# One-hot rows of two edge pairs built by one comparison against a row in PSUM, in a three-layer relational GNN on one Trainium2 core

## Chip, cores and metric

The kernel runs on one core of one Trainium2 chip. The metric is the device time of one execution, in microseconds. The engines are named as in the profile: PE (TensorE), DVE (VectorE), ACT (ScalarE), POOL (GpSimd) and SP (SyncE); each runs its own instructions in program order and waits on semaphores that other engines or DMAs raise.

## The reference

A graph of 6250 nodes with 256 features and 100000 edges, sorted by target node, with three edge types; three layers, then a layer norm of input plus result.

```
ew = edge_attr @ edge_w + edge_b                       # (100000, 256)
inv_cnt[r] = 1 / max(number of edges of type r into the node, 1)
for l in range(3):
    residual = x
    msg = relu(x[src] * ew)
    out = 0
    for r in range(3):
        h = segment_sum(msg * (edge_type == r), dst)   # (6250, 256)
        out += (h * inv_cnt[r]) @ weights[l, r]
    out += x @ roots[l] + biases[l]
    x = residual + relu(out)
result = layernorm(x_in + x)
```

## The kernel before

**Pairs, quads and steps.** The edges are cut into 391 *pairs* of two times 128 edges; two neighbouring pairs are a *quad* and share one 128x1024 tile of gathered rows, `xs`. A layer walks over its pairs in a fixed order, one pair at a *step* `it`, and the order of every engine's instructions is written out by hand in that loop. There is no scheduler. At step `it` the loop emits, among others and in this order:

- the two gathers of pair `it + 9`: `gather_pair` (L1054), indirect DMAs that POOL issues, 128 rows each; 2346 over the three layers. The quads take turns in eight buffers for `xs`, the *rooms*: the first gather of a quad waits until the quad eight earlier has been reduced;
- `reduce` of pair `it` (L687 where a span is reduced turned, else L695): one-hot times rows, summed over edges into a PSUM bank of `h_pool`, which has two banks;
- `make_ew` (L634, edge weights of a later quad on PE into PSUM `ew_p`, which holds the bias already: `seed_ew`, L621 on ACT), `weigh` (L656 on DVE, `xs` times `ew_p`, and L657 on ACT, the relu), each once in two steps;
- now and then the root term `x @ roots` of a block of 128 nodes: 49 in a layer, one every six steps or more. `root_turn` (L728, two transposes on PE into `r_p`), two steps later `root_turned` (L732, ACT copies them to `t_s`), three steps later `root_mul` (L736, two products on PE into the other half of `r_p`), six steps later `root_keep` (L739, DVE adds the bias);
- `node_mul` and `node_end` (L754, L785, L788) where the sums of a block of nodes are complete: products with the layer's weights into `o_p`, and the update of `x_all`;
- every second step `one_hot` of the quad that is reduced two steps later (L669): four DVE comparisons of 128x120, each of the row `iota_w` (places 0 to 39, three times) in SBUF with one column of `seg`. In the first layer ACT makes a bfloat16 copy `oh_b` (L673);
- last, `add` (L723): DVE adds the finished span of the step before from its bank of `h_pool` to the sums `acc`. Only then can PE open that bank again, with the `reduce` of the step that follows.

**Start and end.** A first part (the *look*) loads the inputs, and finds out whether the edges are sorted; a flag and two branches (L1171 and L1174) choose `ordered_path`, which is described here, or `general_path`, which does not run with these inputs. In `ordered_path` ACT's queue then loads the edge weights' matrix (`ew_sb`) and bias (`seed`, and a third copy, `left`), DVE makes `bias` in bfloat16 parts from `left`, and DVE (one memset, L518) and ACT (two activations, L520) set `acc` to zero. The last layer ends with the norm and the writes of `out` by SP (L808), and then the second branch.

Of the kernel before, what the change touches and what calls it, by code (L numbers as in the profile page):

```python
# [442 lines left out]
def ordered_path(ctx, tc, x, attr_laid, A, weights, roots, biases, edge_w, edge_b, out, src, src_i, seg, place_i, consts, x_root,  # L443
# [6 lines left out]
    nc = tc.nc  # L450
    P = 128
    N, D = x.shape
    E = src.shape[0]
    L, R = weights.shape[:2]
# [3 lines left out]
    U = T // 2  # L458
    assert OCT * A == P
    DC = D // P  # L460
    WK = R * WIN
# [4 lines left out]
    for u, (lo, hi) in enumerate(zip(least, most)):  # L466
# [4 lines left out]
        else:  # L471
            reach.append((0, RING - 1))
    ident, ones, iota_w = consts

# [4 lines left out]
    big = ctx.enter_context(tc.tile_pool(name="big", bufs=1))  # L479
    ew_sb = big.tile([P, 2, D], F32, name="ew_sb")  # L480
    nc.vector.memset(ew_sb, 0.0)
    for j in range(OCT):
        nc.scalar.dma_start(ew_sb[j * A:(j + 1) * A, j % 2, :], edge_w)
    seed = big.tile([P, 2, D], F32, name="seed")
    for i in range(2):
        nc.scalar.dma_start(seed[:, i, :], edge_b[None, :].to_broadcast([P, D]))
    bias = big.tile([PARTS, 2, D], BF, name="bias")
    with tc.tile_pool(name="bias_s", bufs=1) as bias_s:
        left = bias_s.tile([P, D], F32, name="left")
        nc.scalar.dma_start(left, edge_b[None, :].to_broadcast([P, D]))  # L490
        row = bias_s.tile([P, 1], F32, name="row")
        nc.vector.tensor_copy(row, node_i)
        is_row = bias_s.tile([P, PARTS], F32, name="is_row")
        part = bias_s.tile([P, D], BF, name="part")
        rows_of = bias_s.tile([P, D], F32, name="rows_of")
        nc.vector.memset(rows_of, 0.0)
        for k in range(PARTS):
            nc.vector.tensor_scalar(is_row[:, k:k + 1], row, float(k), None, op0=ALU.is_equal)
            nc.vector.tensor_copy(part, left)
            nc.vector.tensor_sub(left, left, part)  # L500
            nc.vector.scalar_tensor_tensor(rows_of, part, is_row[:, k:k + 1], rows_of, op0=ALU.mult, op1=ALU.add)
        for i in range(2):
            nc.vector.tensor_copy(bias[:, i, :], rows_of[:PARTS, :])

# [8 lines left out]
    nc.vector.memset(eps, EPS)  # L513
    full_ones = big.tile([P, P], BF, name="full_ones")
    nc.vector.memset(full_ones, 1.0)
    for c in range(DC + 1):
        if c < DC // 2:
            nc.vector.memset(acc[:, c], 0.0)  # L518
        else:
            nc.scalar.activation(acc[:, c].rearrange("p r n -> p (r n)"),  # L520
                                 zero.to_broadcast([P, R * (ASIDE + 2 * P + WIN)]), AF.Copy)
# [5 lines left out]
    src_r = big.tile(list(src_i.shape), I32, name="src_r")  # L527
    src_e = big.tile([P, 2 * FIRST], I32, name="src_e")
    came = big.tile([P, 2 * FIRST, P], F32, name="came")
    came_i = came.bitcast(I32)  # L530

# [55 lines left out]
    def layer(l, r_sb, b_sb, ats, early, pools):  # L587
# [56 lines left out]
        def complete(q):  # L644
            for k in pairs_of(q):

                rest = (r_pool if k else o_pool).tile([P, 2, D], F32, name="r_p" if k else "o_p")
# [17 lines left out]
        def one_hot(q):  # L665
            ohs[q] = edge.tile([P, 4, WK], F32, name="oh", bufs=3)
            n = 2 * len(pairs_of(q))
            for t in reversed(range(n)):
                nc.vector.tensor_scalar(ohs[q][:, t, :].rearrange("p (r w) -> p r w", r=R), iota_w[:, :, :WIN], seg[:, 4 * q + t:4 * q + t + 1], None,  # L669
                                        op0=ALU.is_equal)  # L670
# [54 lines left out]
        def root_turn(c):  # L725
            rs[c] = r_pool.tile([P, 2, DC * P], F32, name="r_p")
            for d in range(DC):
                nc.tensor.transpose(rs[c][:, 0, d * P:(d + 1) * P], x_all[:, c, d * P:(d + 1) * P], ident)  # L728

        def root_turned(c):  # L730
            t_ss[c] = edge.tile([P, DC, P], F32, name="t_s", bufs=1)
            nc.scalar.activation(t_ss[c], rs[c][:, 0, :], AF.Copy)  # L732

        def root_mul(c):
            for d in range(DC):
                nc.tensor.matmul(rs[c][:, 1, :], t_ss[c][:, d, :], r_sb[:, d, :], start=(d == 0), stop=(d == DC - 1))  # L736

        def root_keep(c):
            nc.vector.tensor_add(x_root[:, at_root[c], :], rs[c][:, 1, :], b_sb)  # L739
            if l == L - 1:  # L740
                nc.vector.tensor_add(x_all[:, c, :], x_all[:, c, :], x0s[c])
# [180 lines left out]
WIN = 40  # L922
# [137 lines left out]
def kernel(ctx, tc, x, src, dst, edge_attr, edge_type, weights, roots, biases, edge_w,  # L1060
# [28 lines left out]
    flag = keep.tile([1, 1], I32, name="flag")  # L1089

    x_root = keep.tile([P, ROOTS, D], F32, name="x_root")

    with tc.tile_pool(name="look", bufs=1) as look, tc.tile_pool(name="look_p", bufs=2, space=PSUM) as look_p, \
# [5 lines left out]
        typ_raw = look.tile([P, TC], I32, name="typ_raw")  # L1099
        nc.sync.dma_start(typ_raw, type_laid)  # L1100

        limits = look.tile([1, 2, U], F32, name="limits")
# [68 lines left out]
    with tc.If(unordered == 0):  # L1171
        ordered_path(tc, x, attr_laid, edge_attr.shape[1], weights, roots, biases, edge_w, edge_b, out, src, src_i, seg, place_i,
                     (ident, ones, iota_w), x_root, first_rows, node_i)
    with tc.If(unordered > 0):  # L1174
        general_path(tc, x, src, dst, edge_attr, edge_type, weights, roots, biases, edge_w, edge_b, out)
# [49 lines left out]
```

## Time and profile before

| | |
|---|---|
| median of 3 runs | 2961.4 us (2960.73 to 2961.57) |
| profiled execution, its own time | 2962.46 us |
| its span in the profile | 2960.2 us |
| mean granted TensorE clock | 0.97 |
| busy share of the span | PE 88%, DVE 68%, ACT 51%, POOL 75% |

Each group row of the profile gives line, engine, operation, output tile <- input tiles, shape and count, then total busy us and mean ns of one, then the engine's idle time ahead of these instructions and what ended it. A timeline row gives start, duration, the instruction, and in square brackets the idle time before it and what ended it. A row of windows gives a stretch, its length, the busy time of PE, PE's weight loads, DVE, ACT and POOL with their counts, then the mean granted clock, the DMA share and GB/s.

### The profile page before, as it was taken

To read this page: it belongs to the slowest core of one execution; us is meant where nothing else is said; L and a number is where in the kernel's file an instruction comes from. 1 tells how busy PE (TensorE), PEld (TensorE's weight loads), DVE (VectorE), ACT (ScalarE), POOL (GpSimd) and SP (SyncE) were. 2 spreads that over 40 slices of the span, in tenths; PEclk is the share of its full clock that TensorE was granted. 3 is DMA by queue.
4 is the path that set the end of the run, shared out by engine and by line. 5 is a ranking of instruction groups with operands and counts; after the bars stand their busy time and mean duration, and the time that the engine had idled before them with its cause. 6 is when DMAs were issued, how large, how long until landed. Compare 5 with 4: busy or idle time off the path is not lost. (4 is left out here: it accounts for less than half of the span.)

```text
span 2960.2 us, 43407 instructions
## 1 busy us (share of the span) xinstructions
PE 2591.9 (88%) x13712; PEld 1782.6 (60%) x13712; DVE 1998.2 (68%) x4910; ACT 1503.8 (51%) x1911; POOL 2228.8 (75%) x2355
## 2 busy tenths in 40 slices
PE   5999999999998878888889998778888888999876
PEld 2666677677765545556666666454555666666644
DVE  6666677778775555566767776545666777888864
ACT  4666656556565444454444444435444444444443
POOL 7777777777777777777777777777777777777776
PEclk9999999999999999999999999889999999999998
DMA  5444444444444444444444444444444444444443
GB/s 168 151 143 136 148 124 125 127 130 130 127 134 128 132 116 120 129 122 124 127 125 130 130 132 129 136 132 125 126 133 133 135 133 132 139 137 137 129 125 97
DMA packets 173705, 387.39 MB, mean 131 GB/s; under 512 B 43594, under 2 KB 79068, under 8 KB 173468
## 3 DMA queue, kind: packets, MB, share of 16 engines
q0 software_dynamic: 112608, 307.65, 36.4%
q1 hardware_dynamic: 53280, 68.50, 7.2%
q10 hardware_dynamic: 7580, 8.37, 1.0%
q8 instruction: 113, 1.85, 0.3%
q14 instruction: 124, 1.02, 0.1%
HBM read 364.89 MB, written 19.46 MB: 130 GB/s over the span
## 5 line engine op out<-in xcount | busy, mean ns | idle before, releaser
L1054 POOL DMA_INDIRECT xs<-x_mid,src_r x1540 | 1460.5, 948 | 469.1 <-issue 363.4
L657 ACT ACTIVATE xs<-xs 128x1024 f32<-128x1024 f32 (+1 forms) x585 | 615.7, 1053 | 1301.0 <-DVE xs L656 1296.5
L656 DVE TENSOR_TENSOR xs<-ew_p,xs 128x1024 f32<-128x1024 f32 (+1 forms) x585 | 711.4, 1216 | 676.7 <-DMA xs<-x_mid,src_r 429.8
L1054 POOL DMA_INDIRECT xs<-in_x_dram,src_io x770 | 732.0, 951 | 234.6 <-issue 192.3
L695 PEld LDWEIGHTS h_p<-oh,xs 128*128 128x128 f32 x5160 | 669.7, 196 | 251.9 <-issue 123.8
L695 PE MATMUL h_p<-oh,xs 128*128 128x120 f32 x5160 | 734.3, 287 | 86.4 <-issue 34.5
L634 PE MATMUL ew_p<-ew_sb,at 64*128 64x512 f32 x2346 | 687.6, 662 | 95.8 <-ACT ew_p L621 92.3
L669 DVE TENSOR_SCALAR oh<-iota_w,seg_o 128x120 f32<-128x120 f32 x2346 | 622.9, 327 | 0.0
L687 PE MATMUL h_p<-xs,oh 128*120 128x256 f32 x2088 | 570.9, 407 | 22.9 <-issue 7.8
L621 ACT ACTIVATE ew_p<-seed 128x1024 f32<-128x1024 f32 x582 | 588.9, 1012 | 0.0
L754 PE MATMUL o_p<-w_sb,acc 128*128 128x256 f32 (+1 forms) x1728 | 440.7, 391 | 28.2 <-DVE x_root L785 24.2
L687 PEld LDWEIGHTS h_p<-xs,oh 128*120 128x120 f32 x2088 | 363.1, 191 | 162.8 <-issue 48.1
L723 DVE TENSOR_TENSOR acc<-h_p,acc 128x240 f32 (+1 forms) x732 | 323.7, 442 | 173.2 <-PE o_p L754 69.6
L754 PEld LDWEIGHTS o_p<-w_sb,acc 128*128 128x128 f32 (+1 forms) x1728 | 309.3, 191 | 152.0 <-DVE x_root L785 62.7
L634 PEld LDWEIGHTS ew_p<-ew_sb,at 64*128 64x128 f32 x2346 | 181.9, 189 | 224.9 <-ACT ew_p L621 121.1
L785 DVE SCALAR_TENSOR_TENSOR x_root<-o_p,inv,x_root 128x256 f32<-128x256 f32 (+1 forms) x432 | 207.0, 479 | 28.3 <-PE o_p L754 21.6
L736 PE MATMUL r_p<-r_sb,t_s 128*128 128x256 f32 x588 | 160.1, 395 | 26.1 <-ACT t_s L732 25.8
L771 ACT ACTIVATE acc<-zero_o 128x768 f32<-128x768 f32 (+1 forms) x150 | 140.2, 934 | 15.3 <-PE o_p L754 14.7
L673 ACT ACTIVATE oh_b<-oh 128x480 bf16<-128x480 f32 x196 | 116.3, 594 | 56.1 <-DVE oh L669 55.2
L728 PEld LDWEIGHTS r_p<-ident_o,x_all 128*128 128x128 f32 x294 | 30.9, 144 | 169.0 <-DVE x_root L739 116.7
L736 PEld LDWEIGHTS r_p<-r_sb,t_s 128*128 128x128 f32 x588 | 103.0, 192 | 47.6 <-ACT t_s L732 36.4
L728 PE MATMUL r_p<-ident_o,x_all 128*128 128x128 f32 x294 | 65.4, 305 | 69.3 <-DVE x_root L739 69.1
(110 smaller groups left out, 940.8 us busy)
## 6 DMA issues: line engine op xcount, KB each, us to landing
at<-in_attr_laid_dram SPq DMA_DIRECT2D x147, 256.0 KB
xs<-x_mid,src_r POOLq DMA_INDIRECT x1540, 2.8
xs<-in_x_dram,src_io POOLq DMA_INDIRECT x770, 2.8
x_mid<-x_all SPq DMA_DIRECT2D x96, 128.0 KB
x_all<-in_x_dram ACTq DMA_DIRECT2D x8, 768.0 KB
x<-in_x_dram SPq DMA_DIRECT2D x48, 128.0 KB
out_dram<-x_all SPq DMA_DIRECT2D x48, 128.0 KB
w_sb<-in_L_gnn_weights_dram SPq DMA_DIRECT2D x3, 768.0 KB
```

The costliest lines, as they stand in the source:

```text
L621: nc.scalar.activation(ew_ps[q][:, :n], seed[:, None, :, :].to_broadcast([P, n, 2, D]), AF.Copy)
L634: nc.tensor.matmul(ew_ps[q][:, k].rearrange("p i d -> p (i d)"), at[half, :], ew_sb[half].rearrange("p i d -> p (i d)"), start=False, stop ...
L656: nc.vector.tensor_mul(there, ew_ps[q][:, pairs.start:pairs.stop], there)
L657: nc.scalar.activation(there, there, AF.Relu)
L669: nc.vector.tensor_scalar(ohs[q][:, t, :].rearrange("p (r w) -> p r w", r=R), iota_w[:, :, :WIN], seg[:, 4 * q + t:4 * q + t + 1], None, o ...
L687: nc.tensor.matmul(h_p[:WK, :D], ohs[u // 2][:, t, :], xs[u // 2][:, u % 2, i, :], start=(i == 0 and first), stop=(i == 1 and closes(u)), ...
L695: nc.tensor.matmul(h_p[:, d * WK:(d + 1) * WK], xs[u // 2][:, u % 2, i, d * P:(d + 1) * P] if d < DC else full_ones, (ohs if d < DC else o ...
L723: nc.vector.tensor_tensor(there, h_ps[span][:, :CH * WK].rearrange("p (c r w) -> p c r w", c=CH, r=R), there, op=ALU.add)
L736: nc.tensor.matmul(rs[c][:, 1, :], t_ss[c][:, d, :], r_sb[:, d, :], start=(d == 0), stop=(d == DC - 1))
L754: nc.tensor.matmul(o_p[:n, j, :], acc[:, d, r, slot:slot + n], w_sb[:, r * DC + d, :], start=(d == 0), stop=(d == DC - 1))
L785: nc.vector.scalar_tensor_tensor(root, o_p[:n, j, :], inv[:n, c, r:r + 1], root, op0=ALU.mult, op1=ALU.add)
L1054: nc.gpsimd.indirect_dma_start(out=xs[:, u % 2, i, :], out_offset=None, in_=x_rows[:, :], in_offset=bass.IndirectOffsetOnAxis(ap=src_i[:, ...
```

## The change

Four things are edited.

1. **One-hots.** `one_hot` makes the one-hot rows of a quad by a single `tensor_tensor` of 128x480 in place of four `tensor_scalar` of 128x120. Its first operand is a row of places, broadcast over the four blocks, that lies in PSUM; its second is four columns of `seg`, broadcast over the places. For the row, `r_pool` becomes one fixed bank, `r_bank`: 256 columns are `r_p`, the next 120 are `places_p`, copied once from `iota_w`. The transposes and the product of a root term now use the same 256 columns one after the other, and the few `node_mul` and `complete` products that took an `r_p` tile take `o_p`, but for one.
2. **Early loads.** `ew_sb` and `seed` are loaded in the look, ahead of the flag; the third copy of the bias is gone, and `bias` is made from `seed` with the tile `came` as scratch.
3. **Zeros.** All three parts of `acc` are set to zero by ACT.
4. **Hint.** In the last layer's last pair a hint names the second branch by its label, `general`.

```
-    ident, ones, iota_w = consts
+    ident, ones, iota_w, ew_sb, seed = consts
...
-    ew_sb = big.tile([P, 2, D], F32, name="ew_sb")
-    nc.vector.memset(ew_sb, 0.0)
-    for j in range(OCT):
-        nc.scalar.dma_start(ew_sb[j * A:(j + 1) * A, j % 2, :], edge_w)
-    seed = big.tile([P, 2, D], F32, name="seed")
...
-        left = bias_s.tile([P, D], F32, name="left")
-        nc.scalar.dma_start(left, edge_b[None, :].to_broadcast([P, D]))
...
+        rest = seed[:, 0, :] if k == 0 else left
+        nc.vector.tensor_scalar(is_row[:, k:k + 1], row, float(k), None, op0=ALU.is_equal)
+        nc.vector.tensor_copy(part, rest)
+        nc.vector.tensor_sub(left, rest, part)
...
     for c in range(DC + 1):
-        if c < DC // 2:
-            nc.vector.memset(acc[:, c], 0.0)
-        else:
-            nc.scalar.activation(acc[:, c].rearrange("p r n -> p (r n)"),
-                                 zero.to_broadcast([P, R * (ASIDE + 2 * P + WIN)]), AF.Copy)
+        nc.scalar.activation(acc[:, c].rearrange("p r n -> p (r n)"),
+                             zero.to_broadcast([P, R * (ASIDE + 2 * P + WIN)]), AF.Copy)
...
     r_pool = ctx.enter_context(tc.tile_pool(name="r_p", bufs=1, space=PSUM))
+    r_bank = r_pool.tile([P, 4 * P], F32, name="r_p")
+    r_p, places_p = r_bank[:, :D], r_bank[:, None, D:D + WK]
+    nc.vector.tensor_copy(r_bank[:, D:D + WK].rearrange("p (r w) -> p r w", r=R), iota_w[:, :, :WIN])
...
-            for t in reversed(range(n)):
-                nc.vector.tensor_scalar(ohs[q][:, t, :].rearrange("p (r w) -> p r w", r=R), iota_w[:, :, :WIN], seg[:, 4 * q + t:4 * q + t + 1], None,
-                                        op0=ALU.is_equal)
+            nc.vector.tensor_tensor(ohs[q][:, :n], places_p.to_broadcast([P, n, WK]),
+                                    seg[:, 4 * q:4 * q + n, None].to_broadcast([P, n, WK]), op=ALU.is_equal)
...
         def root_turn(c):
-            rs[c] = r_pool.tile([P, 2, DC * P], F32, name="r_p")
             for d in range(DC):
-                nc.tensor.transpose(rs[c][:, 0, d * P:(d + 1) * P], x_all[:, c, d * P:(d + 1) * P], ident)
+                nc.tensor.transpose(r_p[:, d * P:(d + 1) * P], x_all[:, c, d * P:(d + 1) * P], ident)
...
-                nc.tensor.matmul(rs[c][:, 1, :], t_ss[c][:, d, :], r_sb[:, d, :], start=(d == 0), stop=(d == DC - 1))
+                nc.tensor.matmul(r_p, t_ss[c][:, d, :], r_sb[:, d, :], start=(d == 0), stop=(d == DC - 1))
...
-            o_p = o_ps[c, part] = (r_pool if part == 1 and c < 2 else o_pool).tile(
-                [P, 2, D], F32, name="r_p" if part == 1 and c < 2 else "o_p")
+            o_p = o_ps[c, part] = r_p[:, None, :] if part == 1 and c == 0 else o_pool.tile([P, 2, D], F32, name="o_p")
...
+            if l == L - 1 and it == U - 1:
+                tc.mark_branch_hint_location("general")
...
+        for i in range(2):
+            nc.scalar.dma_start(seed[:, i, :], edge_b[None, :].to_broadcast([P, D]))
+        for j in range(OCT):
+            nc.scalar.dma_start(ew_sb[j * A:(j + 1) * A, j % 2, :], edge_w)
...
-    with tc.If(unordered > 0):
+    with tc.If(unordered > 0, label="general"):
```

Three places show what moves. The first is DVE in the first layer, around a root product: `L669` of before is the group of four comparisons, `L659` of after the single one; `L723` and `L713` are the `add`, `L656` and `L647` the `weigh`; `PE_49` is the semaphore that PE raises. Before:

```order
L723 TENSOR_TENSOR acc<-h_p,acc 128x9x40 [waits PE_49]
L669 TENSOR_SCALAR oh<-iota_w,seg_o 128x120 x4
L723 ISA
L723 TENSOR_TENSOR acc<-h_p,acc 128x9x40 [waits DVE_49,PE_49]
L656 TENSOR_TENSOR xs<-ew_p,xs 128x1024 [waits DMASW1_49,DMASW2_49,DMASW0_49,DMASW3_49,PE_49,Activation_49]
L716 TENSOR_LOAD place_i
L723 ISA
L723 TENSOR_TENSOR acc<-h_p,acc 128x9x40 [waits DVE_49,PE_49]
L669 TENSOR_SCALAR oh<-iota_w,seg_o 128x120 x4
```

And after:

```order
L713 TENSOR_TENSOR acc<-h_p,acc 128x9x40 [waits PE_49]
L659 TENSOR_TENSOR oh<-r_p,seg_o 128x480 [waits PE_49]
L713 ISA
L713 TENSOR_TENSOR acc<-h_p,acc 128x9x40 [waits DVE_49]
L647 TENSOR_TENSOR xs<-ew_p,xs 128x1024 [waits DMASW2_49,DMASW1_49,DMASW3_49,DMASW0_49,Activation_49]
L706 TENSOR_LOAD place_i
L713 ISA
L713 TENSOR_TENSOR acc<-h_p,acc 128x9x40 [waits DVE_49,PE_49]
L659 TENSOR_TENSOR oh<-r_p,seg_o 128x480 [waits PE_49]
```

The order is the same, but a one-hot waited for nothing before, and now waits for PE: the first of the two for the transposes of a root term (L717), the second for its product (L725). Over the program 137 one-hots wait for transposes and 147, one for each root term, for a product.

The second place is PE at a root product in the first layer (`L736` before, `L725` after), which stands between the end of one `reduce` and the start of the next. Before:

```order
L695 LDWEIGHTS full_ones
L695 MATMUL h_p<-oh_b,full_ones 128x120
L736 MATMUL r_p<-r_sb,t_s 128x256 [waits Activation_49]
L736 MATMUL r_p<-r_sb,t_s 128x256
L695 MATMUL h_p<-oh,xs 128x120 [waits DMASW2_49,DVE_49]
```

And after:

```order
L685 LDWEIGHTS full_ones
L685 MATMUL h_p<-oh_b,full_ones 128x120
L725 MATMUL r_p<-r_sb,t_s 128x256 [waits Activation_49]
L725 MATMUL r_p<-r_sb,t_s 128x256
L685 MATMUL h_p<-oh,xs 128x120 [waits DMASW2_49,DVE_49,PE_49]
```

Nothing moved on PE. The `reduce` in the last row waits for an `add` on DVE, as before; that `add` now stands behind a one-hot that waits for the product in the row above.

The third place is ACT's queue at the start. Before, the loads stood behind the flag and the branch:

```order
L1098 DMA dst_raw<-in_dst_laid_dram 128x782
L1170 TENSOR_LOAD flag [waits DVE_49]
L1171 COMPARE_AND_BRANCH
L486 DMA seed<-in_L_gnn_edge_b_dram 128x256 [waits DMAHW0_49,DVE_49,DMAHW3_49,PE_49,Pool_49]
```

And after:

```order
L1092 DMA dst_raw<-in_dst_laid_dram 128x782
L1097 DMA seed<-in_L_gnn_edge_b_dram 128x256 x2
L1099 DMA ew_sb<-in_L_gnn_edge_w_dram 32x256 [waits DVE_49]
L1099 DMA ew_sb<-in_L_gnn_edge_w_dram 32x256
```

The loads of `seed` and `ew_sb` moved ahead of the flag and wait only for the memset of `ew_sb`.

More of the change, by code (lines that the diff above doesn't have):

```diff
@@ L479, in ordered_path @@
     big = ctx.enter_context(tc.tile_pool(name="big", bufs=1))
-    ew_sb = big.tile([P, 2, D], F32, name="ew_sb")
-    nc.vector.memset(ew_sb, 0.0)
-    for j in range(OCT):
-        nc.scalar.dma_start(ew_sb[j * A:(j + 1) * A, j % 2, :], edge_w)
-    seed = big.tile([P, 2, D], F32, name="seed")
-    for i in range(2):
-        nc.scalar.dma_start(seed[:, i, :], edge_b[None, :].to_broadcast([P, D]))
-    bias = big.tile([PARTS, 2, D], BF, name="bias")
-    with tc.tile_pool(name="bias_s", bufs=1) as bias_s:
-        left = bias_s.tile([P, D], F32, name="left")
-        nc.scalar.dma_start(left, edge_b[None, :].to_broadcast([P, D]))
[L491 to L503, printed above, removed]
@@ new lines, in ordered_path @@
+    src_r = big.tile(list(src_i.shape), I32, name="src_r")
+    src_e = big.tile([P, 2 * FIRST], I32, name="src_e")
+    came = big.tile([P, 2 * FIRST, P], F32, name="came")
+    came_i = came.bitcast(I32)
+    full_ones = big.tile([P, P], BF, name="full_ones")
+    nc.vector.memset(full_ones, 1.0)
+    bias = big.tile([PARTS, 2, D], BF, name="bias")
+    scratch = came.rearrange("p t e -> p (t e)")
+    left, rows_of = scratch[:, :D], scratch[:, D:2 * D]
+    row, is_row = scratch[:, 2 * D:2 * D + 1], scratch[:, 2 * D + 1:2 * D + 1 + PARTS]
@@ new lines, in ordered_path @@
+    part = came.bitcast(BF).rearrange("p t e -> p (t e)")[:, 6 * D:7 * D]
+    nc.vector.tensor_copy(row, node_i)
+    nc.vector.memset(rows_of, 0.0)
+    for k in range(PARTS):
+        rest = seed[:, 0, :] if k == 0 else left
+        nc.vector.tensor_scalar(is_row[:, k:k + 1], row, float(k), None, op0=ALU.is_equal)
+        nc.vector.tensor_copy(part, rest)
+        nc.vector.tensor_sub(left, rest, part)
+        nc.vector.scalar_tensor_tensor(rows_of, part, is_row[:, k:k + 1], rows_of, op0=ALU.mult, op1=ALU.add)
@@ L505, in ordered_path @@
+    for i in range(2):
+        nc.vector.tensor_copy(bias[:, i, :], rows_of[:PARTS, :])
     x_all = big.tile([P, NT, D], F32, name="x_all")
@@ L645, in complete @@
             for k in pairs_of(q):
-                rest = (r_pool if k else o_pool).tile([P, 2, D], F32, name="r_p" if k else "o_p")
+                rest = o_pool.tile([P, 2, D], F32, name="o_p")
                 for i in range(2):
@@ L725, in root_turn @@
         def root_turn(c):
-            rs[c] = r_pool.tile([P, 2, DC * P], F32, name="r_p")
             for d in range(DC):
-                nc.tensor.transpose(rs[c][:, 0, d * P:(d + 1) * P], x_all[:, c, d * P:(d + 1) * P], ident)
+                nc.tensor.transpose(r_p[:, d * P:(d + 1) * P], x_all[:, c, d * P:(d + 1) * P], ident)
         def root_turned(c):
             t_ss[c] = edge.tile([P, DC, P], F32, name="t_s", bufs=1)
-            nc.scalar.activation(t_ss[c], rs[c][:, 0, :], AF.Copy)
+            nc.scalar.activation(t_ss[c].rearrange("p d e -> p (d e)"), r_p, AF.Copy)
         def root_mul(c):
             for d in range(DC):
-                nc.tensor.matmul(rs[c][:, 1, :], t_ss[c][:, d, :], r_sb[:, d, :], start=(d == 0), stop=(d == DC - 1))
+                nc.tensor.matmul(r_p, t_ss[c][:, d, :], r_sb[:, d, :], start=(d == 0), stop=(d == DC - 1))
         def root_keep(c):
-            nc.vector.tensor_add(x_root[:, at_root[c], :], rs[c][:, 1, :], b_sb)
+            nc.vector.tensor_add(x_root[:, at_root[c], :], r_p, b_sb)
             if l == L - 1:
@@ L1089 @@
     flag = keep.tile([1, 1], I32, name="flag")
+    ew_sb = keep.tile([P, 2, D], F32, name="ew_sb")
+    seed = keep.tile([P, 2, D], F32, name="seed")
+    A = edge_attr.shape[1]
     x_root = keep.tile([P, ROOTS, D], F32, name="x_root")
@@ L1172 @@
         ordered_path(tc, x, attr_laid, edge_attr.shape[1], weights, roots, biases, edge_w, edge_b, out, src, src_i, seg, place_i,
-                     (ident, ones, iota_w), x_root, first_rows, node_i)
-    with tc.If(unordered > 0):
+                     (ident, ones, iota_w, ew_sb, seed), x_root, first_rows, node_i)
+    with tc.If(unordered > 0, label="general"):
         general_path(tc, x, src, dst, edge_attr, edge_type, weights, roots, biases, edge_w, edge_b, out)
```

7 lines of the change are left out of this document (1 added, 6 removed).

## The prediction

> **What bounds the kernel now.** I read the page's busy shares first, then the groups of POOL, its waits, three windows, and the first and the last gather.
>
> ```profile
> span 2960.2 us, 43407 instructions
> PE 2591.9 (88%) x13712; PEld 1782.6 (60%) x13712; DVE 1998.2 (68%) x4910; ACT 1503.8 (51%) x1911; POOL 2228.8 (75%) x2355
> L1054 POOL DMA_INDIRECT xs<-x_mid,src_r x1540 | 1460.5, 948 | 469.1 <-issue 363.4
> L1054 POOL DMA_INDIRECT xs<-in_x_dram,src_io x770 | 732.0, 951 | 234.6 <-issue 192.3
> ```
>
> ```profile
> POOL xs L1054 <- issue: 562.1, 1845, 0.3
> ```
>
> ```profile
> 500.00:600.00 100.00, 94.97 (x609) 69.89 (x608) 77.98 (x189) 60.35 (x76) 75.70 (x80) 1.00 0.44 128
> 900.00:1000.00 100.00, 84.39 (x486) 56.90 (x482) 47.32 (x110) 47.37 (x59) 75.63 (x81) 0.93 0.45 129
> 2700.00:2800.00 100.00, 89.66 (x517) 65.53 (x514) 83.28 (x217) 49.07 (x63) 75.94 (x80) 1.00 0.46 132
> ```
>
> ```profile
> 3.81 1.12 POOL L1054 DMA_INDIRECT x_root<-in_x_dram,src_f  x1 [1.44 <-DMA src_f<-in_src_laid_dram]
> 2944.28 0.95 POOL L1054 DMA_INDIRECT xs<-x_mid,src_r  x1 [0.30 <-issue]
> 2954.73 0.34 SPq L808 DMA_DIRECT2D out_dram<-x_all  x1
> ```
>
> By busy share PE leads with 88% and POOL has 75%, but POOL's idle time is all of one kind: 0.3 us of issue between one gather and the next, 1845 times. A gather of 0.949 us and 0.30 us of issue are 1.25 us, and 100 us hold 80 of these in every window, whether PE is busy for 84 or 95 us and DVE for 47 or 83. From 3.81 to 2944.28 us stand 2345 periods of 1.254 us (2940.5 / 2345). So POOL is at its limit from end to end, and the span is 3.8 us of head, 2940.5 us of gathers, and 15.9 us from the start of the last gather to the end. What another engine gains in between is worth nothing; what it loses costs nothing until POOL has to wait for a room. So the second question is how much margin the rooms have, from the last product of the reduce that frees a room to the first gather that uses it, eight quads later (pairs counted along the order):
>
> ```profile
> 477.94 0.66 PE L695 MATMUL h_p<-oh,xs 128*128 128x120 f32 x4
> 501.48 0.95 POOL L1054 DMA_INDIRECT xs<-in_x_dram,src_io  x1 [0.30 <-issue]
> 815.85 0.66 PE L695 MATMUL h_p<-oh,xs 128*128 128x120 f32 x4
> 825.05 0.95 POOL L1054 DMA_INDIRECT xs<-in_x_dram,src_io  x1 [0.30 <-ACT xs L657]
> ```
>
> At 500 us the margin is 501.48 - 478.60 = 22.9 us; at 825 us it is 825.05 - 816.51 = 8.5 us. In the first layer PE falls behind POOL by 14 us in 320 us, and 8.5 us is the least margin of that stretch. That is what this change has to be held against.
>
> **The change part by part.** *The one-hots, and their new wait.* The places of the quads lie in the same bank as the root term's results, and the one-hot of a step in which a root product stands now waits for that product. Today it waits for nothing. One such place, in the first layer:
>
> ```profile
> 640.80 1.06 DVE L669 TENSOR_SCALAR oh<-iota_w,seg_o 128x120 f32<-128x120 f32 x4
> 641.78 0.52 DVE L723 TENSOR_TENSOR acc<-h_p,acc 128x360 f32 x1
> 644.67 1.08 PE L736 MATMUL r_p<-r_sb,t_s 128*128 128x256 f32 x4
> 645.60 0.60 PE L695 MATMUL h_p<-oh,xs 128*128 128x120 f32 x4
> 644.45 1.22 DVE L656 TENSOR_TENSOR xs<-ew_p,xs 128x1024 f32<-128x1024 f32 x1 [2.15 <-DMA xs<-in_x_dram,src_io]
> 645.59 0.99 DVE L785 SCALAR_TENSOR_TENSOR x_root<-o_p,inv,x_root 128x256 f32<-128x256 f32 x2
> 646.62 0.42 DVE L788 SCALAR_TENSOR_TENSOR x_all<-x_root,x_all 128x256 f32<-128x256 f32 x1
> 647.42 0.53 DVE L723 TENSOR_TENSOR acc<-h_p,acc 128x360 f32 x1 [0.38 <-issue]
> 648.01 0.70 PE L695 MATMUL h_p<-oh,xs 128*128 128x120 f32 x4
> ```
>
> DVE makes the one-hot at 640.80, some 4 us before PE's product, and right behind it the add at 641.78, which frees the bank that PE opens at 645.60. In the changed kernel the one-hot starts when the product has ended, and the add behind it; PE's next reduce, which follows the product without a gap today, waits for both. The four rows of weighing, update and add behind it wait too, on DVE. The length of the one-hot and the price of an add that comes late:
>
> ```profile
> L669 DVE TENSOR_SCALAR oh<-iota_w,seg_o 128x120 f32<-128x120 f32 x2346 | 622.9, 327 | 0.0
> 2947.08 0.42 DVE L662 TENSOR_TENSOR xs<-ew_p,xs 128x256 f32<-128x256 f32 x1 [0.25 <-DMA xs<-x_mid,src_r]
> 2944.82 0.69 DVE L656 TENSOR_TENSOR xs<-ew_p,xs 128x512 f32<-128x512 f32 x1 [0.22 <-ACT xs L657]
> 758.47 0.53 DVE L723 TENSOR_TENSOR acc<-h_p,acc 128x360 f32 x1 [3.00 <-PE o_p L754]
> 759.06 0.70 PE L695 MATMUL h_p<-oh,xs 128*128 128x120 f32 x4 [0.63 <-DVE acc L723]
> 417.11 0.70 PE L695 MATMUL h_p<-oh,xs 128*128 128x120 f32 x4 [1.60 <-DVE acc L723]
> ```
>
> A tensor_tensor with one operand in PSUM takes 0.42 us for 256 columns and 0.69 for 512, so 0.66 for 480 (0.42 + 224 x 0.27/256), against 1.06 for four comparisons: DVE gains 0.4 us in a quad. An add that can only begin when PE's last product has ended costs PE 0.63 us (758.47 began so). With the one-hot ahead of it, an event costs 0.63 + 0.66 = 1.29 us. The least it can cost is 0.63, if the one-hot found its way ahead; the most that a late add costs in the rows is 1.60. I take 1.29, because both parts are rows of the same operations.
>
> How many events? The stretch between 220 and 776 us has
>
> ```profile
> 220.00:776.00 556.00, 40.30 (x148) 25.23 (x148) 0.99 0.45 131
> ```
>
> 148 matmuls of L736 (count in the third column), four to a root, so 37 root products. Counted along PE's order in the changed program, 30 of the first layer's products are followed at once by a reduce that waits for the add of the step; in five, node products stand between, which hide 1.29 us; the others are early ones before 220 us or wait for nothing new. So 30 x 1.29 = 38.7 us of new waits on PE. Against that stand PE's old waits for adds:
>
> ```profile
> PE h_p L695 <- DVE acc L723: 9.5, 12, 1.6
> PE h_p L687 <- DVE acc L723: 3.6, 4, 2.5
> ```
>
> These are the waits from 220 to 620 us, where PE runs right behind the gathers (margin 22.9) and its lateness comes from rows that arrive late. A PE that is late for another reason finds those adds done: I take off the 9.5 us whole. The four waits of 3.6 us lie where turned spans are reduced; each shrinks by the 0.4 us of a shorter one-hot, 1.6 us together. PE's net loss by 825 us is 38.7 - 9.5 - 1.6 = 27.6 us. The room margin takes 8.5 of it, and POOL has to wait for the rest: **19.1 us**. Later gathers run on from there; the lost time isn't won back, since POOL has no slack. Bounds: 30 x 0.63 = 18.9, less 11.1, is 7.8 us, under the margin, so 0; 30 x 1.60 = 48, less 9.5 and 8.5 (without the gain of 1.6), is +30.
>
> In the second and third layers (the window at 2700 us) PE is idle for 8 to 10 us in 100, with some 22 such products in a layer of 980 us. 22 x 1.29 = 28 us of waits against about 90 us of idle time: cover enough, cost 0. Without it those layers would add up to 28 us each.
>
> [...]
>
> *Early loads and zeros.* Today bias arrives late:
>
> ```profile
> 33.49 1.01 PE L630 MATMUL ew_p<-bias,full_ones 3*128 3x512 bf16 x2 [18.07 <-DVE bias L503]
> 25.99 3.60 ACT L520 ACTIVATE acc<-zero_o 128x4080 f32<-128x4080 f32 x1
> 21.27 3.46 DVE L518 MEMSET acc<- 128x4080 f32 x1 [0.80 <-issue]
> ```
>
> PE can begin its first edge weights perhaps 9 us earlier, and ACT takes on 3.6 us of zeros for DVE's 3.46. POOL gathers since 3.81 us through all this without a gap, so both are worth 0: earlier consumers only widen the first margin. The six loads now stand ahead of ACT's own flag and branch; at the 0.34 us that SP's issue of a load takes in the row above they delay ACT by 2 us at most, less than the 9 us it gains, and POOL reads its flag on its own queue.
>
> *Hint.* At the end SP stands for 2.6 us at the second branch, while the last output rows, issued at 2954.73 us and after, still travel:
>
> ```profile
> SPq L1174 <- SPq L1174: 2.6, 1, 2.6
> ```
>
> A hint can take away between 0 and 2.6 us; the landing of those rows is near, so I take 1.6.
>
> *The sum.* Against the profiled execution: 2962.5 + 19.1 - 1.6 = 2980.0 us (its span 2960.2 and 2.3 us around it). The median of the runs is 1.1 us lower, and the forecast is for the median: 2961.4 + 19.1 - 1.6 = **2978.9 us**.
>
> **The rivals.** *R1, POOL never waits: not slower.* If an event costs PE under 0.65 us, the net loss (30 x 0.65 - 11.1 = 8.4) stays within the margin of 8.5 us, and only the hint counts: 2961.4 - 1.6 = 2959.8 us. For it: the price of 0.63 is a row, and adds elsewhere come earlier by a faster DVE. Against it: for 0.63 the one-hot would have to cost nothing after the product, and the place shown has DVE idle or early, not PE. This is the point that decides: 0.65 us of PE's wait for an event.
>
> *R2, shorter gathers: faster.* The one-hots read SBUF alone; a read from PSUM could leave POOL a freer path. If each of the 2346 gathers fell from the mean of 0.949 us to 0.94, that is 2346 x 0.009 = 21 us, and with the hint 2938.8 us, provided the rooms hold no gather. Against it:
>
> ```profile
> 40.83 1.06 DVE L669 TENSOR_SCALAR oh<-iota_w,seg_o 128x120 f32<-128x120 f32 x4
> 40.94 0.94 POOL L1054 DMA_INDIRECT xs<-in_x_dram,src_io  x1 [0.30 <-issue]
> ```
>
> This gather lies wholly beside a one-hot and takes 0.94 us, no more than any other; and the windows hold 80 gathers at any DVE load. [...]
>
> *R3, DVE doesn't recover: still slower.* In the place shown, DVE would end the add behind the one-hot at 645.75 + 0.66 + 0.53 = 646.9, then needs 1.22 + 0.99 + 0.42 + 0.53 = 3.2 us up to the add that frees PE's next bank, 650.1 us; PE, itself late by 1.29, wants it at 649.3. That is another 0.8 us. If every event had it, 30 x 2.09 = 62.7, less 11.1 and 8.5, is 43 us: 3003 us. Against: only events with a node update behind them have it, and the next add there waits for other things anyway.
>
> **How the numbers follow.** A measurement of this kernel can tell about 0.2% (5.9 us) from no change: faster is under 2955.5 us, slower over 2967.3. The forecast, POOL held for 6 to 35 us, has 0.60: the wait is in the program, its size is from rows, and the margin of 8.5 us is small beside it. R1 has 0.28, as the lower price alone is enough for it. R2 has 0.06 and R3 (over 2996 us) 0.06. So faster 0.06, same 0.28, slower 0.66. The range goes from 2958.5 us (R1 with the whole hint, 2.6 us off, rounded) to 2996 (1.60 us an event, 30 us, and some of R3); it leaves out the ends of R2 and R3, 0.12, and a little at its own edges. The forecast's own range is 2967 to 2996.
>
> **What would show it.** Right: in the changed kernel's trace POOL's gathers wait for a PE reduce between 600 and 850 us, together 15 to 25 us, and nowhere later; the one-hot row lasts about 0.66 us; DVE idles ahead of it for PE's root product, and PE waits 1.2 to 1.4 us for an add right behind 30 root products of the first layer; the 100 us windows of layers two and three hold 80 gathers as before; the end after the last gather is 1 to 2 us shorter. Wrong: gathers back to back throughout (R1); gathers of 0.94 us or less on average (R2); gathers held in the later layers too, or second waits of PE behind each event (R3); a one-hot well over 1 us, which would make every step's add late, not only those at root products.

## The result

The changed kernel takes 2990.4 us (median of 4 runs, 2990.1 to 2990.8) against 2961.5 us before: a ratio of 1.0097, with a 95% interval of 1.0079 to 1.0114. The forecast was 2978.9 us, in a range of 2958.5 to 2996.0. It is slower, by 28.9 us (1.0%) where 17.5 were forecast.

From the page of the kernel after, the rows that answer to those of before (L1044 is the gather, L659 the one-hot):

```profile
span 2988.4 us, 41290 instructions
PE 2588.1 (87%) x13712; PEld 1771.8 (59%) x13712; DVE 1759.4 (59%) x3152; ACT 1506.7 (50%) x1912; POOL 2229.5 (75%) x2355
L1044 POOL DMA_INDIRECT xs<-in_x_dram,src_io x770 | 732.5, 951 | 261.9 <-issue 221.3
L659 DVE TENSOR_TENSOR oh<-r_p,seg_o 128x480 f32<-128x480 f32 x588 | 382.1, 650 | 517.8 <-PE r_p L725 410.9
```

DVE works 239 us less than before (1759 against 1998), and the kernel is slower. A gather is as long as before. POOL's idle time ahead of the first layer's gathers has grown from 234.6 to 261.9 us, and the one-hots, which had no idle time ahead of them, now have 517.8 us. Windows of the kernel after:

```profile
500.00:600.00 100.00, 91.81 (x587) 67.21 (x586) 64.84 (x121) 56.73 (x69) 73.95 (x79) 1.00 0.43 123
700.00:800.00 100.00, 91.20 (x578) 67.70 (x576) 66.27 (x124) 55.31 (x68) 67.90 (x71) 1.00 0.41 117
900.00:1000.00 100.00, 92.51 (x523) 62.25 (x523) 49.73 (x69) 63.87 (x80) 75.63 (x81) 0.98 0.46 133
2700.00:2800.00 100.00, 91.92 (x538) 67.81 (x538) 76.83 (x162) 49.70 (x64) 75.64 (x81) 1.00 0.46 135
```

From 700 to 800 us POOL issues 71 gathers where it issued 80; after the first layer's root terms it runs at its full rate again. The same place as in the prediction, the root product that stood at 644.67 us, first DVE's rows and then PE's, from the timeline of the kernel after:

```profile
671.75 0.66 DVE L659 TENSOR_TENSOR oh<-r_p,seg_o 128x480 f32<-128x480 f32 x1 [4.95 <-PE r_p L725]
672.32 0.52 DVE L713 TENSOR_TENSOR acc<-h_p,acc 128x360 f32 x1
675.73 0.53 DVE L713 TENSOR_TENSOR acc<-h_p,acc 128x360 f32 x1 [0.34 <-issue]
```

```profile
670.62 1.09 PE L725 MATMUL r_p<-r_sb,t_s 128*128 128x256 f32 x4
672.94 0.68 PE L685 MATMUL h_p<-oh,xs 128*128 128x120 f32 x4 [1.23 <-issue]
676.37 0.68 PE L685 MATMUL h_p<-oh,xs 128*128 128x120 f32 x4 [1.09 <-issue]
```

DVE stands for 4.95 us until the product has ended at 671.71, makes the one-hot and the add, and PE's next reduce begins 1.23 us after the product. The profile writes "issue" there; the add ended at 672.84, 0.10 us ahead of PE's start, and by the order shown under "The change" this reduce waits for it. At this place a second wait follows (1.09 us, for the add at 675.73), as the rival R3 had it.

The waits of DVE and of PE from 220 to 830 us in the kernel after:

```profile
DVE oh L659 <- PE r_p L725: 141.2, 37, 5.7
DVE oh L659 <- PE r_p L717: 41.3, 30, 2.4
```

```profile
PE h_p L685 <- issue: 27.0, 22, 1.5
PE h_p L677 <- issue: 12.9, 10, 1.6
PE h_p L685 <- DVE acc L713: 9.7, 15, 1.2
```

All 37 root products of the stretch hold a one-hot. Taken product by product from PE's rows, 29 of them are followed by a wait, 26 of these of 1.23 or 1.24 us; together 36.7 us, where the same places had 1.5 us before. At the other eight, PE goes on with node products and does not wait behind the root product. All other gaps of PE, counted in PE's order from 220 us to the reduce at 815.85 us of before, fell only from 22.1 to 19.2 us. The room that was closest to late before, in the kernel after:

```profile
851.21 0.66 PE L685 MATMUL h_p<-oh,xs 128*128 128x120 f32 x4
852.63 0.96 POOL L1044 DMA_INDIRECT xs<-in_x_dram,src_io  x1 [2.31 <-ACT acc L759]
```

This reduce now begins 851.21 - 815.85 = 35.4 us later than before, and the gather follows its end (851.87) by 0.76 us, which is the least that is seen in this trace: POOL waits for the room. So the usable margin was 8.5 - 0.8 = 7.8 us, and 35.4 - 7.8 = 27.6 us is what POOL was held; 852.63 - 825.05 gives the same 27.6. The end:

```profile
2972.29 0.95 POOL L1044 DMA_INDIRECT xs<-x_mid,src_r  x1 [0.31 <-issue]
2982.75 0.34 SPq L796 DMA_DIRECT2D out_dram<-x_all  x1
SPq L1173 <- SPq L1173: 2.7, 1, 2.7
```

The last gather starts 28.0 us later than before, and the stretch behind it is 16.1 us against 15.9: the rest of the difference isn't there, and SP stands at the second branch for as long as before.

### The profile page after: what moved, and what is told of

It is laid out like the page before. It is cut to its first block, busy times and chain, and to the rows that moved or that the text cites. A ratio compares the mean times of both kernels' runs of the same rounds, so it can differ in the third digit from the quotient of the medians.

```text
span 2988.4 us, 41290 instructions
## 1 busy us (share of the span) xinstructions
PE 2588.1 (87%) x13712; PEld 1771.8 (59%) x13712; DVE 1759.4 (59%) x3152; ACT 1506.7 (50%) x1912; POOL 2229.5 (75%) x2355
## 5 line engine op out<-in xcount | busy, mean ns | idle before, releaser
L1044 POOL DMA_INDIRECT xs<-x_mid,src_r x1540 | 1460.8, 949 | 469.1 <-issue 387.5
L647 DVE TENSOR_TENSOR xs<-ew_p,xs 128x1024 f32<-128x1024 f32 (+1 forms) x585 | 710.0, 1214 | 467.0 <-DMA xs<-x_mid,src_r 304.8
L1044 POOL DMA_INDIRECT xs<-in_x_dram,src_io x770 | 732.5, 951 | 261.9 <-issue 221.3
L685 PE MATMUL h_p<-oh,xs 128*128 128x120 f32 x5160 | 726.6, 286 | 123.4 <-issue 79.6
L685 PEld LDWEIGHTS h_p<-oh,xs 128*128 128x128 f32 x5160 | 658.8, 194 | 292.8 <-issue 188.5
L659 DVE TENSOR_TENSOR oh<-r_p,seg_o 128x480 f32<-128x480 f32 x588 | 382.1, 650 | 517.8 <-PE r_p L725 410.9
L742 PE MATMUL o_p<-w_sb,acc 128*128 128x256 f32 (+1 forms) x1752 | 447.4, 392 | 28.9 <-DVE x_root L773 25.8
L713 DVE TENSOR_TENSOR acc<-h_p,acc 128x240 f32 (+1 forms) x732 | 324.2, 443 | 137.5 <-PE o_p L742 74.8
L725 PE MATMUL r_p<-r_sb,t_s 128*128 128x256 f32 x588 | 157.2, 390 | 16.1 <-ACT t_s L721 15.9
L725 PEld LDWEIGHTS r_p<-r_sb,t_s 128*128 128x128 f32 x588 | 102.7, 191 | 34.1 <-ACT t_s L721 23.0
L717 PEld LDWEIGHTS r_p<-ident_o,x_all 128*128 128x128 f32 x294 | 31.2, 144 | 136.0 <-DVE x_root L728 75.4
L717 PE MATMUL r_p<-ident_o,x_all 128*128 128x128 f32 x294 | 64.8, 303 | 39.3 <-DVE x_root L728 39.1
```

The source lines that it names most:

```text
L647: nc.vector.tensor_mul(there, ew_ps[q][:, pairs.start:pairs.stop], there)
L659: nc.vector.tensor_tensor(ohs[q][:, :n], places_p.to_broadcast([P, n, WK]), seg[:, 4 * q:4 * q + n, None].to_broadcast([P, n, WK]), op=ALU ...
L685: nc.tensor.matmul(h_p[:, d * WK:(d + 1) * WK], xs[u // 2][:, u % 2, i, d * P:(d + 1) * P] if d < DC else full_ones, (ohs if d < DC else o ...
L713: nc.vector.tensor_tensor(there, h_ps[span][:, :CH * WK].rearrange("p (c r w) -> p c r w", c=CH, r=R), there, op=ALU.add)
L725: nc.tensor.matmul(r_p, t_ss[c][:, d, :], r_sb[:, d, :], start=(d == 0), stop=(d == DC - 1))
L742: nc.tensor.matmul(o_p[:n, j, :], acc[:, d, r, slot:slot + n], w_sb[:, r * DC + d, :], start=(d == 0), stop=(d == DC - 1))
```

## The experiments

**One-hot ahead of the root term.** The call of `one_hot` moves in the step's code, and with it DVE's order.

```
+            if pair(2) is not None and first_of(it + 2, 2) and pair(2) // 2 != order[-1] // 2:
+                one_hot(pair(2) // 2)
             if it - 3 in root_at:
                 root_mul(root_at[it - 3])
...
-            if pair(2) is not None and first_of(it + 2, 2) and pair(2) // 2 != order[-1] // 2:
-                one_hot(pair(2) // 2)
```

> The changed kernel, with the one-hot of a step emitted ahead of the root term's transposes and product instead of behind them, so that DVE's one-hot no longer waits for PE's product (PE's product waits for the one-hot instead, which DVE has made some 4 us earlier). Theory (the wait at the root products is the whole loss): PE's waits right behind a root product are gone, POOL's gathers are never held, the margin of the rooms stays over 8 us, and the time is 2960 to 2963 us. Rival 1 (the longer comparison or its operand in PSUM costs by itself): 2985 us or more. Rival 2 (DVE falling behind, not the add): between, 2970 to 2980.

2964.8 us, ratio 1.0015 (1.0006 to 1.0025): 25 of the 29 us are back with the same comparison, the same row in PSUM and the same shared bank. So the operand in PSUM is not what costs, and rival 1 falls. (The code puts the one-hot behind the transposes and ahead of the product; the expectation names both.) The theory's own figures were missed by a little: the ten runs go from 2962.7 to 2971.3 us, and PE was still 8.2 us later than before at the end of the root terms, all of the margin. The waits of DVE show what was left:

```profile
DVE oh L659 <- PE r_p L717: 48.4, 33, 3.4
```

**The transposes one step later too,** behind that step's one-hot.

```
-            if it in root_at:
-                root_turn(root_at[it])
...
+            if it - 1 in root_at:
+                root_turn(root_at[it - 1])
             if it - 3 in root_at:
                 root_mul(root_at[it - 3])
```

> The changed kernel with the one-hot ahead of the root product, as in the first experiment, and the root term's transposes one step later, behind that step's one-hot, so that a one-hot comes two steps after them. Theory (the 8.2 us that PE still lost in the first experiment are one-hots held by the transposes, and PE's transposes and products held behind DVE): PE's lateness falls under 4 us, no gather is held, 2960 to 2962 us. Rival (the copy of the transposes by ACT and the product come too close together): PE waits for t_s, 2963 us or more.

2962.6 us, ratio 0.9999 (0.9990 to 1.0009). PE's lateness at the end of the root terms is 0.0 us, and the last gather starts when it did before:

```profile
2944.28 0.95 POOL L1044 DMA_INDIRECT xs<-x_mid,src_r  x1 [0.30 <-issue]
```

So the remaining 8.2 us hang on the place of the transposes; this run does not tell the one-hots that they held from PE's own work held behind DVE, as the move changes both. One-hots still wait here, for ACT's copy of the transposes (30.0 us, 32 times, from 220 to 830 us), and that costs nothing. With the waits for PE gone, DVE's 239 us of saved work bring nothing either, as POOL sets the time.

**Old comparisons, everything else of the change kept.**

```
-            nc.vector.tensor_tensor(ohs[q][:, :n], places_p.to_broadcast([P, n, WK]),
-                                    seg[:, 4 * q:4 * q + n, None].to_broadcast([P, n, WK]), op=ALU.is_equal)
+            for t in reversed(range(n)):
+                nc.vector.tensor_scalar(ohs[q][:, t, :].rearrange("p (r w) -> p r w", r=R), iota_w[:, :, :WIN], seg[:, 4 * q + t:4 * q + t + 1], None,
+                                        op0=ALU.is_equal)
```

> The changed kernel with the four comparisons against the row in SBUF as before; early loads, zeros by ACT, the shared bank for the root term and the branch hint stay. Theory: 2961 to 2962 us, the same as before, since POOL gathers from end to end and the hint left the last stretch after the last gather at 16.1 us against 15.9. Rival (one of the other edits carries part of the loss): 2965 us or more.

2960.9 us, ratio 1.0000 (0.9990 to 1.0009). The whole loss is in the one-hots; early loads, zeros and the hint are worth nothing that can be measured.

**Add ahead of the one-hot.**

```
+            for span in add_at.get(it, ()):
+                add(span)
             if pair(2) is not None and first_of(it + 2, 2) and pair(2) // 2 != order[-1] // 2:
                 one_hot(pair(2) // 2)
...
-            for span in add_at.get(it, ()):
-                add(span)
```

> The changed kernel, with the add of a step ahead of its one-hot. The one-hot still waits for the root product, so DVE is held as in the changed kernel, but the add that PE's next reduce needs is no longer behind it. Theory (the price is the add that stands behind the held one-hot, 1.25 us an event): the waits behind the products go, 2961 to 2965 us. Rival (DVE's lost lead is what costs: weighing and node updates late): 2975 us or more, with PE's waits spread over other adds.

2965.5 us, ratio 1.0017 (1.0008 to 1.0027), at the upper edge of the theory's range. DVE is still held by root products (91.4 us, 32 times, from 220 to 830 us), and PE's waits behind the products are gone but for three. So most of the price was the add behind the held one-hot. PE was still 10.5 us late at the end of the root terms, in waits elsewhere (34.5 us of other gaps against 22.1 before): a held DVE alone costs about that much, most of it inside the margin.

**At every second root term only.** The call stands ahead of the product where the index of the root term is even.

```
+            ahead = it - 3 in root_at and sorted(root_at).index(it - 3) % 2 == 0
+            if ahead:
+                make_one_hot(pair)
             if it - 3 in root_at:
                 root_mul(root_at[it - 3])
...
+            if not ahead:
+                make_one_hot(pair)
```

> The changed kernel with the one-hot ahead of the root product at every second root term only. PE fell behind the kernel before by 35.4 us at the end of the first layer's root terms in the changed kernel, and by 8.2 us with all one-hots ahead. Theory (a fixed price for each held one-hot, less the margin of the rooms): (35.4 + 8.2) / 2 = 21.8 us late, 7.8 us of that in the margin, POOL held for 14 us, 2975 to 2976 us. Rival (a few places carry the loss, or DVE recovers between): under 2968 or over 2984 us.

2969.4 us, ratio 1.0024 (1.0014 to 1.0034), between the theory and the rival. In the stretch 17 products are followed by waits, 20.8 us in all; PE's lateness was 14.5 us, not the mean of 21.8, and 14.5 - 7.8 = 6.7 us is what POOL lost. The margin's arithmetic holds; the halving doesn't, since the first waits are partly taken up by gaps that PE had anyway (others fell from 22.1 to 16.4 us), and more of them aren't (19.2 us in the changed kernel).

**Nine rooms.**

```
-ROWS = 8
+ROWS = 9
```

> The changed kernel with nine rooms for gathered rows instead of eight. Theory (POOL is held only for what PE's lateness exceeds the rooms' margin): one quad more, four gathers of 1.254 us, is 5.0 us of margin, so POOL is held for 27.5 - 5.0 = 22.5 us, 2985.4 us. Rival (POOL's wait has another cause than the rooms): 2990 us.

2987.6 us, ratio 1.0085 (1.0068 to 1.0102): 2.8 us better than the changed kernel instead of 5.0. At the end of the first layer's held stretch the gathers were 4.2 us ahead of the changed kernel's; later 1.7 us went again, 1.3 of them in gathers that were a little longer on the mean in that run. The sign and most of the size fit the rooms; the rest isn't settled.

**Row in SBUF.**

```
-    r_p, places_p = r_bank[:, :D], r_bank[:, None, D:D + WK]
-    nc.vector.tensor_copy(r_bank[:, D:D + WK].rearrange("p (r w) -> p r w", r=R), iota_w[:, :, :WIN])
+    places_s = big.tile([P, WK], F32, name="places_s")
+    r_p, places_p = r_bank[:, :D], places_s[:, None, :]
+    nc.vector.tensor_copy(places_s.rearrange("p (r w) -> p r w", r=R), iota_w[:, :, :WIN])
```

> The changed kernel with the row of places in SBUF instead of PSUM: one comparison of 128x480 with both inputs in SBUF, no bank shared with the root term. Theory of the wait alone: no one-hot waits for PE, 2961 us. Rival (a DVE operation with two SBUF inputs lengthens the gathers beside it, as the few longer gathers of the kernel before lie beside such operations): gathers beside one-hots of 1.0 us and more, a period over 1.254 us, 2980 to 3010 us.

3014.8 us, ratio 1.0184 (1.0167 to 1.0201). No one-hot waits here, and none of the rooms holds a gather; the gathers themselves are longer, from the groups and the timeline of this kernel:

```profile
L660 DVE TENSOR_TENSOR oh<-places_s,seg_o 128x480 f32<-128x480 f32 x588 | 380.8, 648 | 0.0
L1045 POOL DMA_INDIRECT xs<-x_mid,src_r x1540 | 1495.9, 971 | 469.2 <-issue 365.9
581.12 0.65 DVE L660 TENSOR_TENSOR oh<-places_s,seg_o 128x480 f32<-128x480 f32 x1
581.41 1.18 POOL L1045 DMA_INDIRECT xs<-in_x_dram,src_io  x1 [0.30 <-issue]
```

The gather that begins while a one-hot with two SBUF inputs runs takes 1.18 us. In this run 284 gathers begin so. They take 1.128 us on the mean, the other 2062 take 0.950, and what counts is how much of the one-hot is still to come: 0.945 us with under 0.1 us left, 1.376 with over 0.5. On the mean of all 2346 gathers 0.9713 instead of 0.9493 us makes 51.7 us. The length of the one-hot is the same, 0.648 and 0.650 us. So in these runs the row in PSUM did avoid something (0.9496 us on the mean in the changed kernel), but the four comparisons of before avoided it too: their gathers take 0.949 us.

**The comparison twice at root products,** to double what PE waits for.

```
+            for _ in range(times):
+                nc.vector.tensor_tensor(ohs[q][:, :n], places_p.to_broadcast([P, n, WK]),
+                                        seg[:, 4 * q:4 * q + n, None].to_broadcast([P, n, WK]), op=ALU.is_equal)
...
+                one_hot(pair(2) // 2, 2 if it - 3 in root_at else 1)
```

> The changed kernel with the comparison made twice, the second time with the same result, in the steps in which a root product stands, and nowhere else. Theory (PE waits for one-hot and add, 0.65 and 0.6 us, behind each of 32 root products of the first layer): each event costs 0.65 us more, 32 x 0.65 = 20.8 us, 3011 us. Rival (the price is the exchange of signals between PE and DVE, or hidden elsewhere): 2991 to 3000 us.

3041.3 us, ratio 1.0276 (1.0255 to 1.0297): 51 us over the changed kernel, not 21. The waits are as forecast: 29 products with a wait, 26 of them of 1.93 us (1.24 + 0.65 and 0.04) and three of 2.18, 56.6 us against 36.7. The other half of the loss isn't in waits. PE's clock shows it, in the windows and the timeline of this kernel:

```profile
720.46 1.08 PE L726 MATMUL r_p<-r_sb,t_s 128*128 128x256 f32 x4
723.47 0.76 PE L686 MATMUL h_p<-oh,xs 128*128 128x120 f32 x4 [1.93 <-issue]
```

```profile
718.20:721.60 3.40, 3.34 (x20) 2.07 (x18) 1.66 (x5) 3.25 (x4) 1.95 (x3) 1.00 0.35 102
721.60:725.00 3.40, 1.53 (x9) 1.51 (x10) 2.87 (x4) 1.07 (x2) 1.82 (x2) 0.84 0.63 205
725.00:728.40 3.40, 3.40 (x12) 1.23 (x11) 0.00 (x0) 1.51 (x2) 1.90 (x2) 0.66 0.16 48
728.40:731.80 3.40, 2.77 (x26) 2.53 (x26) 3.03 (x6) 0.94 (x2) 1.89 (x2) 1.00 0.35 99
240.00:880.00 640.00, 562.90 (x3314) 398.96 (x3312) 397.59 (x712) 343.53 (x441) 432.60 (x456) 0.97 0.40 117
```

Behind the wait of 1.93 us the granted clock falls for about 3.4 us, with 12 matmuls where a stretch of that length holds 20 or more. Eleven of the 29 waits are followed by such a fall, one of them of twice that length; over the 640 us the clock is 0.97. All gaps of PE from 220 us to the end of the root terms are 79.0 us against 55.9, and PE's rows between them take 595.4 us against 575.4; 23 + 20 are the 43 us by which the first layer is longer than in the changed kernel. Of the other 7 us, 5 come in the third layer near 2810 us, where the rooms now hold four gathers; the rest comes little by little between. In the changed kernel the same stretch has the full clock:

```profile
240.00:860.00 620.00, 565.32 (x3444) 406.81 (x3442) 389.14 (x703) 354.37 (x453) 448.87 (x473) 1.00 0.43 126
```

**Half of that dose.** The second comparison covers 240 columns.

```
-            for _ in range(times):
+            for m in (n, n // 2)[:times]:
```

> The changed kernel with the comparison made a second time for half of its columns (240), with the same result, in the steps in which a root product stands. With the whole second comparison each event cost 0.65 us more of waiting, as forecast, but PE's granted clock fell to 0.84 and 0.66 in the 3.4 us stretches of and after a wait of 1.93 us, some 20 us in all, and the time went up by 51 us. The half makes a wait of about 1.25 + 0.42 = 1.67 us. Theory A (the clock falls only behind waits of some 1.9 us): 30 x 0.42 = 13 us, 3003 us, with the clock at 1.00 from 240 to 880 us. Theory B (the clock falls in proportion, or already at 1.6 us): 3012 us or more, with windows under 1.00.

3016.5 us, ratio 1.0189 (1.0172 to 1.0206), with runs from 3012.0 to 3018.0. Of its 29 waits 26 are of 1.68 us and three of 2.17, together 50.2 us. In the profiled run of 3012.0 us the clock fell in three of the 20 us windows from 240 to 880 us, one of them

```profile
260.00:280.00 20.00, 18.32 (x89) 12.14 (x91) 10.85 (x19) 10.37 (x15) 15.13 (x17) 0.91 0.54 165
259.89 0.66 PE L678 MATMUL h_p<-xs,oh 128*120 128x256 f32 x2 [2.17 <-issue]
```

so some 5 us were lost to the clock. Two of the three falls, the one shown among them, stand behind waits of 2.17 us; only the third, at 527.0 us, stands behind one of 1.68. So theory A's clock of 1.00 is not met, but 25 of the 26 waits of 1.68 us left the clock alone, and theory B's fall in proportion is not seen either, though the time lies where B put it. In the trace 13.4 us of waits behind products, 2.2 of other gaps and 5.1 of clock make up all but 1 of the 21.7 us over the changed kernel. The other three runs, 3 to 6 us longer, left no trace, and what they lost is open.

## Why the prediction was right, and where its sizes were off

**What bounds the kernel** was right: POOL's gathers set the time, and a change counts only where it holds them. The run with the wait taken out and DVE lighter by over 200 us ties with the kernel before.

**The mechanism** was right, at its place: one-hots held by root products, adds behind them, PE's reduces behind these, rooms freed late, POOL held in the first layer between 580 and 860 us and nowhere later (27 us, where 15 to 25 us between 600 and 850 were named). The single steps: the one-hot 0.65 us (0.66 forecast), an event 1.24 us (1.29), 29 events (30), their sum 36.7 us with 1.5 that stood there before (38.7).

**The step that was mis-sized** is what was set against these waits: 9.5 + 1.6 = 11.1 us of credit for PE's old waits, and nothing for new ones. My reason was that a PE that is late for another reason finds those adds done. At twelve places, five of them in the stretch that the 9.5 us come from, this can't be: the add waits there for PE's own node products, DVE stands idle until they end, and PE's wait of 0.62 to 0.70 us is the same before and after, 7.6 us in all. The prediction's own rows at 758.47 and 759.06 us are such a place. After:

```profile
792.65 0.53 DVE L713 TENSOR_TENSOR acc<-h_p,acc 128x360 f32 x1 [1.07 <-PE o_p L742]
793.24 0.70 PE L685 MATMUL h_p<-oh,xs 128*128 128x120 f32 x4 [0.63 <-DVE acc L713]
```

At all old places together, of any kind, the gaps still shrank by 9.6 us. But 18 new ones came up, 6.5 us in all: two second waits of 1.08 and 1.09 us, the latter at 676.37 us, and sixteen of 0.19 to 0.66 us, whose cause stays open. So the other gaps fell by 3.0 us instead of 11.1. A term left out is PE's rows themselves, which take 2.8 us more (575.4 against 572.5). This fits reduces that no longer overlap what stands before them: at 645.60 us before, the reduce began 0.15 us ahead of the product's end, and after it begins 1.23 us behind it. With the 0.3 us by which PE was late at 220 us already, 0.3 + 36.7 - 1.5 - 3.0 + 2.8 = 35.3 us is the measured lateness of 35.4 within rounding. Of the margin of 8.5 us 0.76 can't be used, and 35.4 - 7.8 = 27.6 stands in the place of 19.1.

That the time still lies in the range is partly luck: its upper end was made for events of 1.60 us and some of R3, and events of 1.24 us came near it only with these other terms.

**The hint** was forecast at 1.6 us, and is worth 0. The 2.6 us at SP's second branch are not the branch: SP passes it 0.2 us after it has issued the last output rows, and then waits 2.7 us for a semaphore, with the hint as without. The likely reading is the landing of those rows, the bound that I had named; I had given it only 1 us of the 2.6. A run with the hint alone wasn't made.

**Early loads and zeros** were forecast at 0, and the run with old comparisons shows 0.

**The rivals.** R1 needed under 0.65 us an event; it is 1.24. R2 needed shorter gathers: they take 0.9496 us on the mean against 0.9493. R3 is seen at two new places, not at every event. The waits of the one-hots for the root term stand in the program; their price is what the runs show, 1.24 us of PE behind a product, and that it hangs on the order of the code: with the one-hot and the transposes moved, the same sharing of a bank costs nothing (2962.6 us). What the kernel would do without these waits, no run tells.

## What to carry to other kernels

An operand moved to a bank that another engine writes can take on that engine's timetable, as here, where all 37 root products from 220 to 830 us held a one-hot, for 141.2 us: look for what stands behind the new wait on its own queue, since here it was less the one-hot than the add behind it that cost the time. When one engine runs back to back, measure the margin of the buffers that it refills, take off a new delay only what that margin holds, and give old waits no credit without a reason for each: one in which the other engine itself waits for this one stays, however late this one is. A wait that can't be removed may be turned round by emitting the early reader ahead of the late writer: here that gave back 25 of 29 us.

## What the hardware showed

**Clock.** In each of the eleven traces all falls of TensorE's granted clock, to one half, begin on one grid of 3.41 us (the 44 of the kernel before and the 35 of the changed kernel within 0.02 us), and nearly all last one stretch of it or two (42 of these 44, 32 of these 35). Cut along that grid, the traces hold 2088 stretches between 220 and 880 us that were not slowed themselves. All 15 in which PE was busy for less than 0.45 of the time, by the profile's modelled ends, were followed by a fall, 8 of the 36 from 0.45 to 0.55, and none of the 2037 others. The one such stretch of the kernel before goes from 317.85 to 321.26 us: PE was busy for 1.43 of its 3.41 us, with a wait of 2.52 us, and in the next one the clock is 0.50. So in these runs a fall followed where enough of a wait fell into one stretch of the grid, and the length of a wait alone did not settle it: 10 of 26 waits of 1.93 us were followed by a fall, 1 of 26 of 1.68 us, and none of 26 of 1.23 or 1.24 us.

**Gathers and DVE.** In the run with the row in SBUF, a gather that began while DVE's comparison of two inputs in SBUF ran was longer (1.18 us instead of 0.95 in the row shown, 1.128 on the mean of 284). In the kernel before the same is seen at 27 gathers that begin under the update of `x_all` from two tiles in SBUF: 1.049 us on the mean. With one of the inputs in PSUM it is not seen there: gathers that begin under the weighing (559) or the add (201) take 0.946 us, like those under the comparisons with a column (476) and those under nothing (851).
